# Split products in the first part's layer two, and a gather of the second part's rows in one stretch

## The chip, the core and the metric

The kernel runs on one core of a Trainium2 chip. The time is device microseconds of one execution, from launch to end; the figure for a kernel is the median of its runs. A separate execution was recorded by the hardware profiler, and all views of the trace come from that one.

## What is computed

The reference is one transformer block on x of shape (8, 1024, 512), float32: an attention whose queries, keys and values are sines and cosines of angles, and then a mixture of experts on the normalised result. Only the second half matters here:

```python
probs = softmax(x @ Wr + br)                 # E = 8 experts
topk_p, topk_e = top_k(probs, 2)
cap = 160                                    # places for each expert and batch entry
buf = scatter rows of x to (expert, batch, place)          # (8, 1280, 512)
h = relu(einsum('enc,ech->enh', buf, W1) + b1)             # 512 -> 2048
y = einsum('enh,ehc->enc', h, W2) + b2                     # 2048 -> 512
out = x + sum over a token's two places of gate * y
```

## The kernel before

**Parts.** Each expert has 1280 rows, taken as a part of 768 rows and a part of 512: sixteen parts, numbered from 0 (`chunks`). A part is cut in two halves of 384 or 256 rows, so `nh`, the number of row blocks of 128 in a half, is 3 or 2. For each part, layer one makes `hid` from the gathered rows (`xe` and its sums `xe_s`), then layer two makes the output rows `y` from `hid` and `w2`, and these are scaled by their gates and added to the output in memory by indirect DMA. All matrix products are float32, and a matmul instruction of the program shows as two records in the profile.

**Products.** Both layers multiply 2 by 2 blocks with seven products in place of eight. The price is sums of blocks. For `w2` they are made by `mix_w2` (VectorE, L1070, 32 instructions for an expert); for layer one's weights by `mix_w1` (L1233); for the rows by the last lines of `gather` (L1200 to L1203).

**Layer two** has three forms. `layer2` (L1372) takes one row block and runs the seven products plainly, each as eight matmuls of 256 columns. `layer2_quad` serves the 512-row parts. `layer2_six` serves 768-row parts from the third part on: product one of blocks 0 and 1 runs plainly (`pair_product`, L1540), the other six are split once more by the class `Second` into seven chains of four matmuls of 128 columns (L1491), and block 2 runs by `layer2`, a step at a time, between them (`some(1, extra)`). Each split product needs eight more sums of 128x512 on VectorE, four of weights (L1460) and four of rows (L1471), written by `both()` two products ahead. `run` then issues the chains, with copies out of PSUM on ScalarE (L1500 to L1515) and additions on VectorE (L1507 to L1513). The six run in the order 5, 6, 2, 3, 7, 4. Their sums alternate between two sets of room: the tiles `xe` and `xe_s`, and three `t1` tiles with `xg`.

The first part (i = 0) does not use it. Its three blocks run one after the other by `layer2`.

**Order.** The order of instructions on TensorE, VectorE, ScalarE and SP is the order in which the program writes them. Work of the next part is woven in by generators: `gather(i + 1, room)` is the generator `aside`, of which `some(n, aside)` or `next(aside)` writes n steps. POOL issues the indirect DMAs: the slot scatters (L773), the row gathers in `fetch` (L1097), and the sends of output rows (L1336).

**Rows.** `fetch` gathers 128 rows to SBUF, `put_row` (SP, L1108) writes them back to memory as `rows_d`, and `quarters` (SP, L1117) reads them again in four loads in a layout that VectorE turns with a 32 by 32 transpose (L1187). For the second part `find_rows(1)` (L1085) computes the row numbers from the slots, four blocks are fetched into the room of `xe_s`, put, and read back into two `z` tiles, two blocks early and two when a `z` comes free. In the first part `find_rows(1)` is written at the ninth step of the layer's 21. For later 512-row parts, `gather` gets `room`, two pieces of `hid` that are no longer read; blocks two and three are read into these.

**Pools** that matter: `ps_p`, six PSUM banks; `gp`, two `z` tiles and one `xg`; `yp`, five `y` tiles of 128x512, each for an output block's rows of one half, free when its send has landed.

Of the kernel before, what the change touches and what calls it, by code (L numbers as in the profile page):

```python
# [22 lines left out]
P = 128  # L23
# [51 lines left out]
def preln_attn_moe_kernel(  # L75
# [110 lines left out]
    room = [t[:, i, :].rearrange("p (i s) -> p i s", i=2) for i in range(2)]  # L186
# [547 lines left out]
    def some(count, *gens):  # L734

        for gen in gens:
            while count and next(gen, 0) is None:
                count -= 1
# [342 lines left out]
    def find_rows(i):  # L1081

        js = slice(chunks[i][1], chunks[i][1] + 2 * chunks[i][2])
        lo, hi = REACH[i]
        nc.vector.tensor_scalar(  # L1085
            source[:, :, js], meta[:, :, js, 0], float(hi * S), float(lo * S),
            ALU.min, ALU.subtract,
        )
# [4 lines left out]
    early = {}  # L1093

    def fetch(i, j, xg):
        e, j0, _ = chunks[i]
        ins = nc.gpsimd.indirect_dma_start(  # L1097
            out=xg, out_offset=None, in_=xn2_d[i % 2],
            in_offset=bass.IndirectOffsetOnAxis(ap=source[:, e, j0 + j, None], axis=0),
        )  # L1100
        if i in (1, 2):
            tc.keep_in_program_order(ins)
        return xg

    def put_row(i, j, xg):
        if i not in rows_d:
            rows_d[i] = dram.tile([2 * chunks[i][2] * P, D], F32, name=f"rows_d{i}")
        nc.sync.dma_start(rows_d[i][j * P : (j + 1) * P, :], xg)  # L1108
# [4 lines left out]
    def quarters(i, j, z):  # L1113

        src = rows_d[i].rearrange("(t g r) (a f) -> t a r g f", r=QUAD, g=NG, a=NG)[j]
        for a in range(NG):
            nc.sync.dma_start(  # L1117
                by_groups(z)[a * QUAD : (a + 1) * QUAD], src[a]
            )
        return z  # L1120
# [4 lines left out]
    def new_z():  # L1125
        return pools["gp"].tile([P, D], F32, name="z")
# [10 lines left out]
    def gather(i, room=None):  # L1137

        e, j0, nh = chunks[i]
        if i == 0:  # L1140
            there = []

            t = row2.tile([P, NCH, 2 * P], F32, name="xT", bufs=1).rearrange("p c t -> p (c t)")
            places = [row2.tile([P, D], F32, name="xn2") for _ in range(2)]
            places += [t[:, :D], t[:, D:]]
            there = [fetch(0, j, xg) for j, xg in enumerate(places)]
            yield None
            there += [fetch(0, 4, new_xg()), fetch(0, 5, new_z())]
        if room:
            spots = room  # L1150
            there = early.pop(i) + [quarters(i, j, room[j - 2]) for j in range(2, 2 * nh)]
            yield None
        xe = pools["xep"].tile([P, NCH, 2, HALF], F32, name="xe")

        def sums():
            return pools["xep"].tile([P, 3, 2, HALF], F32, name="xe_s")

        if not room:
            s = sums()
            spots = s.rearrange("p k c n -> p (k c n)")  # L1160
            spots = [spots[:, k * D : (k + 1) * D] for k in range(4)]
        if i == 1:
            for j, xg in enumerate(spots):
                put_row(1, j, fetch(1, j, xg))
            early[1] = [quarters(1, j, new_z()) for j in range(2)]
            yield None
        if i and not room:
            there = early.pop(i)
            if i > 1:
                there += [quarters(i, j, spots[j - 2]) for j in range(2, 2 * nh)]  # L1170
            yield None
            yield None
        for j in range(2 * nh):
            if j:
                yield None
            xg = there[j]
            dst = xe[:, :, j // nh, j % nh * P : (j % nh + 1) * P]
            if i == 0:
                ps = two_banks()[:, :, : NCH * 64]
                for c in range(NCH):  # L1180
                    by_halves(ps[:, :, c * 64 : (c + 1) * 64], xg[:, c * P : (c + 1) * P])
                nc.vector.tensor_copy(
                    dst.rearrange("p c (a q) -> p c a q", a=2),
                    ps.rearrange("p a (c q) -> p c a q", q=64),
                )
            else:
                nc.vector.transpose(  # L1187
                    dst.rearrange("p k (g j) -> p k g j", j=QUAD),
                    by_groups(xg).rearrange("p g (r k) -> p k g r", k=NCH),
                )  # L1190
            if len(there) < 2 * nh:
                there.append(quarters(i, len(there), new_z()))
        if room:
            yield None
            s = sums()
        n = nh * P
        a11, a12 = xe[:, :2, 0, :n], xe[:, 2:, 0, :n]
        a21, a22 = xe[:, :2, 1, :n], xe[:, 2:, 1, :n]
        s2, s3, s4 = (s[:, k, :, :n] for k in range(3))
        TT(s3, a11, a21, ALU.subtract)  # L1200
        TT(a21, a21, a22, ALU.add)
        TT(s2, a21, a11, ALU.subtract)
        TT(s4, a12, s2, ALU.subtract)  # L1203
        yield a11, a12, s4, a22, a21, s2, s3

    def behind(count, gen):
        for _ in range(count):
            yield
        yield from gen

    def later_on(do, *args):
        do(*args)
        yield

    def start(gen, box):
        for box[0] in gen:
# [140 lines left out]
    def new_y():  # L1357
        y = pools["yp"].tile([P, D], F32, name="y")
        return y, y[:, :DC], y[:, DC:]
# [164 lines left out]
    two = range(2)  # L1524
# [20 lines left out]
    def layer2_six(i, hid, aside, mix_next):  # L1545
# [28 lines left out]
        some(1, extra)  # L1574
        add_to(y11, second[2].run(c))
        second[7].both()
        three = second[3].run(c)
        for b in two:
            TT(as_pair(y12[b]), five[b], three[b], ALU.add)
# [9 lines left out]
        for b in two:  # L1589
            TT(as_pair(y22[b]), five[b], seven[b], ALU.add)  # L1590
        TT(c6, c6, c, ALU.add)
        some(1, aside)
        four = second[4].run(c5, lambda: some(2, aside), lambda: some(1, aside))
        for b in two:
            TT(as_pair(y21[b]), six[b], four[b], ALU.add)
# [106 lines left out]
    def experts(ending):  # L1702
# [5 lines left out]
        for i, (e, j0, nh) in enumerate(chunks):  # L1708
# [28 lines left out]
                    mixes = mix_w2(0)  # L1737
            rest(mixes)
            rest(ahead)
            room = [hid[:, 4 * h : 4 * h + 4, 0, :P] for h in range(2)] if i and nh > 2 else None  # L1740
            aside = start(gather(i + 1, room), box) if i + 1 < len(chunks) else iter(())
            if i == 0:

                aside = itertools.chain(behind(8, later_on(find_rows, 1)), aside)

            def mix_next():
                if i + 1 < len(chunks):
                    mix_w1(i + 1, 0)

            if i and nh > 2:  # L1750
                layer2_six(i, hid, aside, mix_next)
            elif i:
                layer2_quad(i, hid, second, aside, mix_next)
            else:
                for block in range(nh):
                    if block == nh - 1:
                        mix_next()
                    for _ in layer2(i, block, hid):
                        next(aside, None)
            rest(aside)  # L1760
            if i % 2 and e + 1 < E:
                load_b2(e + 1)
# [242 lines left out]
```

## Time and profile before

| | us |
|---|---|
| median of three runs | 3160.34 |
| lowest and highest | 3158.16, 3162.79 |
| profiled execution | 3160.96 |
| its span, first to last instruction | 3159.2 |
| TensorE busy in the span | 3085.4 |
| VectorE busy | 2393.9 |
| ScalarE busy | 1686.1 |
| first part's layer two, first matmul to the second part's first | 1333.95 to 1407.25 |
| third part's layer two, likewise | 1573.89 to 1642.61 |
| mean granted TensorE clock | 0.998 of full |

In the lines of the profile, PE is TensorE, PEld its weight loads, DVE VectorE, ACT ScalarE, POOL GpSimd, SP SyncE; a q behind the name is the engine's queue, which waits or issues. A line of the timeline gives the start, the time to the end of the last one, the engine, the line of the code, the operation, what is written and read, the shape, and how many there are in a row; in brackets the idle time before it and what ended it. A line of the windows gives for a stretch its length and for each engine the busy time and the number of instructions, then the granted TensorE clock, the mean share of the DMA engines and GB/s. Ends of matmuls are modelled, so lengths of TensorE's work are taken from start to start.

### The profile page before, as it was taken

What the parts mean: (1) busy time and instruction counts of PE and PEld (TensorE: products, weight loads), DVE (VectorE), ACT (ScalarE), POOL (GpSimd) and SP (SyncE); (2) the same over time, 40 slices, a digit from 0 to 9 for tenths busy, and PEclk for the clock granted to TensorE, in tenths of its full rate; (3) what the DMA queues carried; (4) which work ended last, traced back from release to release, by engine and by line L of the source; (5) the groups of instructions that cost most, each with busy time, mean ns of one, the idle gap of its engine ahead of it and who ended that gap; (6) DMA issues with size and microseconds to landing.
All of it is one profiled execution on the core that took longest, in us unless ns stands there. A gap on an engine that the chain in (4) does not pass through costs nothing.

```text
span 3159.2 us, 53457 instructions
## 1 busy us (share of the span) xinstructions
PE 3085.4 (98%) x20422; PEld 2149.6 (68%) x20422; DVE 2393.9 (76%) x4962; ACT 1686.1 (53%) x2672; POOL 421.3 (13%) x387
## 2 busy tenths in 40 slices
PE   5999999999999999999999999999999999999998
PEld 2454444544444544689699699699698698698697
DVE  8888888888888776738678678677777777777775
ACT  7888888888788885413423423423423423423423
POOL 3000202010101122320110110010110010110110
PEclk9999999999999999999999999999999999999999
DMA  5435454544545352433523523523523523423421
GB/s 168 148 101 167 110 165 133 156 135 147 155 140 161 81 168 63 142 84 96 156 52 92 156 50 99 155 50 99 150 54 102 142 57 105 135 57 108 133 46 22
DMA packets 288559, 358.86 MB, mean 114 GB/s; under 512 B 28376, under 2 KB 199088, under 8 KB 276272
## 3 DMA queue, kind: packets, MB, share of 16 engines
q1 hardware_dynamic: 264944, 312.20, 33.4%
q0 software_dynamic: 22912, 43.22, 7.5%
q8 instruction: 162, 2.65, 0.4%
q14 instruction: 93, 0.76, 0.1%
q10 hardware_dynamic: 448, 0.02, 0.0%
HBM read 207.02 MB, written 81.22 MB: 91 GB/s over the span
## 4 chain that ended last, share of the span: by engine, by line
PE 75%; ACT 12%; DVE 7%; DMA 3%; issue 2%; SPq 0%; POOLq 0%; POOL 0%; ACTq 0%; DVEq 0%
PE ps_p L1258 30%; PE ps_p L1491 13%; PE ps_s L688 8%; PE ps_p L1372 8%; PE ps_p L1540 7%; PE av L722 7%; ACT e L708 6%; ACT qk_c L598 1%; DMA xn_d<-xn 1%; ACT t_r L449 1%; PE ps_s L216 1%; ACT qk_r L449 1%; ACT L598 1%; DMA qk<-qk_r 1%; ACT L1908 1%
## 5 line engine op out<-in xcount | busy, mean ns | idle before, releaser
L688 PE MATMUL ps_s<-qk 64*128 64x512 f32 (+3 forms) x3072 | 584.6, 503 | 31.3 <-ACT e L708 13.7
L708 ACT ACTIVATE e<-ps_s 128x1024 f32<-128x1024 f32 (+1 forms) x640 | 554.4, 944 | 73.4 <-PE ps_s L702 45.3
L722 PE MATMUL av<-e,v 128*64 128x512 f32 (+3 forms) x3072 | 509.5, 488 | 0.0
L688 PEld LDWEIGHTS ps_s<-qk 64*128 64x128 f32 x3072 | 261.1, 188 | 219.1 <-ACT e L708 105.9
L722 PEld LDWEIGHTS av<-e,v 128*64 128x64 f32 x3072 | 206.0, 137 | 278.9 <-issue 258.5
L1258 PE MATMUL ps_p<-xe,w 128*128 128x256 f32 (+1 forms) x1024 | 317.6, 433 | 1.1 <-issue 1.1
L1258 PE MATMUL ps_p<-xe_s,t 128*128 128x256 f32 (+1 forms) x1024 | 317.7, 433 | 0.0
L1258 PE MATMUL ps_p<-xe,t 128*128 128x256 f32 (+1 forms) x1024 | 317.7, 433 | 0.0
L1336 POOL DMA_INDIRECT out_dram<-y,slots x80 | 127.6, 1595 | 1237.2 <-ACT y L1331 956.8
L773 POOL DMA_INDIRECT slot_d<-token,slot x128 | 153.6, 1200 | 1026.2 <-issue 627.2
L1258 PEld LDWEIGHTS ps_p<-xe_s,t 128*128 128x128 f32 x1024 | 194.4, 190 | 81.4 <-issue 0.8
L1258 PEld LDWEIGHTS ps_p<-xe,t 128*128 128x128 f32 x1024 | 194.2, 190 | 80.4 <-issue 0.4
L1258 PEld LDWEIGHTS ps_p<-xe,w 128*128 128x128 f32 x1024 | 193.7, 190 | 79.4 <-issue 1.2
L1301 DVE TENSOR_TENSOR hid<-hid 128x256 f32<-128x256 f32 (+1 forms) x128 | 63.5, 496 | 199.3 <-ACT hid L1299 199.1
L1258 PE MATMUL ps_p<-xe_s,w 128*128 128x256 f32 (+1 forms) x512 | 158.9, 433 | 0.6 <-ACT p L1274 0.6
L1372 PE MATMUL ps_p<-w,hid 128*128 128x256 f32 x640 | 142.9, 379 | 0.0
L1491 PE MATMUL ps_p<-w,hid 128*128 128x128 f32 x1104 | 141.8, 275 | 0.0
L702 PEld LDWEIGHTS <-keys_b 64*128 64x128 bf16 x1536 | 78.7, 95 | 91.1 <-issue 72.4
L730 DVE TENSOR_SCALAR av_sb<-av,inv_o 128x512 f32<-128x512 f32 x128 | 94.4, 746 | 57.7 <-PE av L722 57.6
L1491 PEld LDWEIGHTS ps_p<-w,hid 128*128 128x128 f32 x1104 | 135.3, 192 | 1.9
L1372 PEld LDWEIGHTS ps_p<-w,hid 128*128 128x128 f32 x640 | 121.1, 190 | 16.4
L1268 ACT COPY hid<-ps_p 128x256 f32<-128x256 f32 (+1 forms) x128 | 53.9, 421 | 139.4 <-PE ps_p L1258 127.4
(314 smaller groups left out, 5502.3 us busy)
## 6 DMA issues: line engine op xcount, KB each, us to landing
w<-in_L_ffn_W_dram SPq DMA_DIRECT2D x256, 256.0 KB, 3.5
w<-in_L_ffn_W_dram SPq DMA_DIRECT2D x64, 512.0 KB, 6.6
qk<-qk_c SPq DMA_DIRECT2D x124, 256.0 KB, 4.6
qk<-qk_r SPq DMA_DIRECT2D x120, 256.0 KB, 5.2
qk_base<-base_d SPq DMA_DIRECT2D x28, 1024.0 KB, 6.5
xn_d<-xn SPq DMA_DIRECT2D x72, 256.0 KB, 2.4
rows_d<-xg SPq DMA_DIRECT2D x70, 256.0 KB, 2.1
x_mid<-in_L_attn_x_dram SPq DMA_DIRECT2D x16, 1024.0 KB, 9.9
```

The lines of the kernel that those rows point to most:

```text
L688: nc.tensor.matmul(ps[:, a, at : at + w], lhsT=pair[r, 1, kb * P : (kb + 1) * P], rhs=pair[r, 0, q0 : q0 + w], start=at == 0, stop=not own ...
L702: nc.tensor.matmul(out_, lhsT=keys_b[r, part, :], rhs=late, start=False, stop=part == 1, skip_group_check=True,)
L708: nc.scalar.activation(e, ps[:, :, :n], AF.Exp, scale=UNIT * UNIT / math.sqrt(2 * DH))
L722: nc.tensor.matmul(av[a * 64 : (a + 1) * 64, q0 - 512 * h :], lhsT=vt[:, kb, 2 * pr + a, :], rhs=es[i][:, a, at : at + w], start=kb == 0, ...
L730: nc.vector.tensor_scalar(av_sb, av, inv_o[:, q : q + 1], None, ALU.mult)
L773: queued = nc.gpsimd.indirect_dma_start(out=slot_d[b], out_offset=bass.IndirectOffsetOnAxis(ap=idx, axis=0), in_=src, in_offset=None,)
L1258: nc.tensor.matmul(ps, lhsT=weights[:, k, :], rhs=rows[:, k, :], start=first and k == 0, stop=last and k == 1, skip_group_check=True,)
L1301: TT(g1, g3, h22, ALU.add)
L1336: ins = nc.gpsimd.indirect_dma_start(out=out, out_offset=bass.IndirectOffsetOnAxis(ap=meta[:, e, jj[r], 0:1], axis=0), in_=y, in_offset=No ...
L1372: nc.tensor.matmul(ps, lhsT=hid[:, k, part, cols], rhs=ws[weight][:, k, :], start=first and k == 0, stop=last and k == NHQ - 1, skip_group ...
L1491: nc.tensor.matmul(ps, lhsT=left[:, k, :], rhs=right[:, k, :], start=first and k == 0, stop=k == 3, skip_group_check=True,)
L1540: nc.tensor.matmul(of(ps, b), lhsT=hid[:, k, part, b * P : (b + 1) * P], rhs=ws[weight][:, k, :], start=first and k == 0, stop=last and k ...
```

## The change

The first part's layer two now goes through `layer2_six` as that of the other 768-row parts does. `gather` for the second part gets `room` as well: at its first step it computes the row numbers, fetches four blocks one after the other (two into `z` tiles, two into `y` tiles), puts them, reads blocks zero and one back into `z` and blocks two and three into the two pieces of `hid`. The step is written behind the sums of product seven. In `layer2_six` the first step of `aside` moves to that place for all parts, from behind product seven's additions; the other steps stay where they are.

```diff
         if room:
-            spots = room
+            if i == 1:
+                find_rows(1)
+                for j in range(2 * nh):
+                    put_row(1, j, fetch(1, j, new_z() if j < 2 else new_y()[0]))
+                early[1] = [quarters(1, j, new_z()) for j in range(2)]
             there = early.pop(i) + [quarters(i, j, room[j - 2]) for j in range(2, 2 * nh)]
             yield None
...
-        if i == 1:
-            for j, xg in enumerate(spots):
-                put_row(1, j, fetch(1, j, xg))
-            early[1] = [quarters(1, j, new_z()) for j in range(2)]
-            yield None
...
         second[7].both()
+        some(1, aside)
         three = second[3].run(c)
...
         TT(c6, c6, c, ALU.add)
-        some(1, aside)
         four = second[4].run(c5, lambda: some(2, aside), lambda: some(1, aside))
...
-            room = [hid[:, 4 * h : 4 * h + 4, 0, :P] for h in range(2)] if i and nh > 2 else None
+            room = [
+                hid[:, 4 * h : 4 * h + 4, 0, :P] for h in two
+            ] if nh > 2 else None
             aside = start(gather(i + 1, room), box) if i + 1 < len(chunks) else iter(())
-            if i == 0:
-
-                aside = itertools.chain(behind(8, later_on(find_rows, 1)), aside)
-
             def mix_next():
                 if i + 1 < len(chunks):
                     mix_w1(i + 1, 0)
 
-            if i and nh > 2:
+            if nh > 2:
                 layer2_six(i, hid, aside, mix_next)
-            elif i:
+            else:
                 layer2_quad(i, hid, second, aside, mix_next)
-            else:
-                for block in range(nh):
-                    if block == nh - 1:
-                        mix_next()
-                    for _ in layer2(i, block, hid):
-                        next(aside, None)
```

The helpers `behind` and `later_on`, which only the first part used, are removed.

## The prediction

> **What bounds the kernel now.** I read the page first (busy shares, slices, the chain that ended last), then the windows of two stretches, then the timelines of TensorE, VectorE, POOL and SP there.
>
> ```profile
> PE 3085.4 (98%) x20422; PEld 2149.6 (68%) x20422; DVE 2393.9 (76%) x4962; ACT 1686.1 (53%) x2672; POOL 421.3 (13%) x387
> ...
> PE 75%; ACT 12%; DVE 7%; DMA 3%; issue 2%; SPq 0%; POOLq 0%; POOL 0%; ACTq 0%; DVEq 0%
> ```
>
> TensorE is busy 98% and holds 75% of the chain. From the first expert on it has hardly a gap, so time saved or lost on it in the first part's layer two reaches the end one for one. That stretch is 1333.95 to 1407.25. The same step of the third part (second expert, 768 rows, already in six split products) is 1573.89 to 1642.61. The windows of both (PE, PEld, DVE, ACT, POOL busy, clock, DMA):
>
> ```profile
> 1333.95:1407.25 73.30, 72.78 (x337) 63.76 (x336) 25.88 (x54) 10.15 (x21) 22.68 (x21) 1.00 0.30 65
> 1573.89:1642.61 68.72, 68.72 (x481) 64.95 (x480) 54.72 (x104) 15.30 (x45) 7.34 (x5) 1.00 0.18 32
> ```
>
> The third part is the model of what the first becomes: 68.72 us on a TensorE without a gap, while VectorE does 54.72 us of work instead of 25.88.
>
> **TensorE's work.** For blocks 0 and 1 each of products two to seven loses 16 matmuls of 256 columns and gets seven chains of four matmuls of 128. Each matmul makes two records. The timeline of the third part:
>
> ```profile
> 1573.89 7.07 PE L1540 MATMUL ps_p<-w,hid 128*128 128x256 f32 x32
> 1580.79 1.05 PE L1491 MATMUL ps_p<-w,hid 128*128 128x128 f32 x8
> 1581.68 1.06 PE L1491 MATMUL ps_p<-xe,hid 128*128 128x128 f32 x8
> 1582.58 1.06 PE L1491 MATMUL ps_p<-xe 128*128 128x128 f32 x8
> ```
>
> Start to start, 16 wide matmuls take 6.90 us and a chain 0.893, so a split product takes 6.25. Six times 0.65 is 3.9 us less. Block 0's own small stall goes too (VectorE's sum L1415 holds TensorE, 0.7 us with the restart). Together that is the difference of the windows: 73.30 - 68.72 = **4.6 us gained**, if the sums keep up.
>
> **The sums of product five come late.** VectorE is strictly in order, and the sums (L1460, L1471) stand behind the mixture of the weights (L1070). In the first part the mixture runs on into layer two:
>
> ```profile
> 1343.67 0.43 DVE L1070 TENSOR_TENSOR w_t<-w,w_t 128x256 f32<-128x256 f32 x1
> 1344.02 0.41 DVE L1389 TENSOR_TENSOR y<-y,ps_p 128x256 f32<-128x256 f32 x1
> ```
>
> In the third part it is over before, and the sums start 3 us ahead of TensorE's first split chain (1577.91 against 1580.79):
>
> ```profile
> 1577.91 1.29 DVE L1460 TENSOR_TENSOR xe<-w 128x512 f32<-128x512 f32 x2
> 1579.11 0.69 DVE L1471 TENSOR_TENSOR xe<-hid 128x512 f32<-128x512 f32 x1
> 1579.84 0.69 DVE L1471 TENSOR_TENSOR hid<-hid 128x512 f32<-128x512 f32 x1
> ...
> 1587.19 0.68 DVE L1471 TENSOR_TENSOR xg<-hid,t 128x512 f32<-128x512 f32 x1
> 1587.80 0.28 DVE L1507 TENSOR_TENSOR xe_s<-xe_s,ps_p 128x128 f32<-128x128 f32 x1
> ```
>
> Today nothing splits here, so nobody waits for 1344.02. After the change: product one ends at 1333.95 + 6.90 = 1340.85, the first chain (no sums) at 1341.75. The second needs the fourth sum, done 2.62 us after the first starts (1580.53 - 1577.91): 1344.02 + 2.62 = 1346.64. TensorE stands **4.9 us**. Its third chain needs the sixth sum (3.82 after the start, 1347.84), 0.3 more. Sixteen sums (9.9 us) then stand before the first PSUM addition of product five. It runs at 1353.9; the next addition on VectorE frees ScalarE's last copy of product five, and behind that stand product six's copies. Product six's third chain can start at about 1354.95 instead of 1354.2, 0.75 more. Together **6.0 us lost**. Later sets have slack: product two starts near 1366.3 (1340.85 + 6.0 + two products at 6.25 + 6.90 of block 2) and its sums are done by 1360.
>
> **The fetch in one stretch.** `find_rows(1)` moves behind the sums of product seven. In the third part these end 12.0 us after product two starts (1612.36 - 1600.33), so here at 1378.3, against 1365.73 before. Behind it stand VectorE's additions of product three; the slots landed at 1365.5, so it waits for nothing. POOL's four gathers follow, now ahead of all six sends, which have nothing ready before them. Then SP's four puts and sixteen quarter loads, no longer waiting for z buffers. From the start of a `find_rows` to its first gather is 0.96 us (1165.48 to 1166.44 at the first part), and from there:
>
> ```profile
> 1371.84 1.01 POOL L1097 DMA_INDIRECT xe_s<-xn_d,source  x1 [0.30 <-issue]
> 1373.15 0.97 POOL L1097 DMA_INDIRECT xe_s<-xn_d,source  x1 [0.30 <-issue]
> 1374.43 0.94 POOL L1097 DMA_INDIRECT xe_s<-xn_d,source  x1 [0.30 <-issue]
> ```
>
> ```profile
> 1378.37 0.32 SPq L1108 DMA_DIRECT2D rows_d<-xe_s  x1
> ```
>
> The third put leaves 6.5 us after the first gather and lands 2.1 us later (the row rows_d<-xg of the DMA list): 1379.2 + 6.5 + 2.1 = 1387.8.
>
> That put matters because row blocks two and three now sit in y buffers. The pool has five; three are in use, these two fill it, and block 2's second y, next in order, inherits the first of them. In the built order of the changed kernel ScalarE's copy into it (L1395) waits for exactly that put. In the third part this copy runs at 1613.20, here it could at 1379.2, so ScalarE stands 8.6 us. Queued behind it: the copy L1397, two gates of block rows 0 and 1, and product seven's first copy, 0.27 + 0.27 + 0.62 + 0.62 + 0.27 = 2.05 us, done at 1389.8. TensorE's third chain of product seven waits for that copy and is due at 1366.3 + 21.2 = 1387.5. **2.3 us lost**. Bounds: the gather lands in 3.2 to 7.7 us and the put in 1.9 to 9.5, so 1 to 6; I take the pace of the same four rows, being nearest.
>
> The rows themselves are in time: first transpose 12.3 us after the first gather (1384.11 - 1371.84), at 1391.5, and it is wanted behind product seven's additions, after 1395. So I cost the sixteen quarter loads and SP's later w1 loads at nothing; the cover is some 4 us. In later parts only the moment of one step's writing moves; its loads keep their place in SP's queue and wait for TensorE's reading of `hid` (84.7 us over seven waits): 0.
>
> **The clock.** Windows around the two places where the granted clock fell:
>
> ```profile
> 58.00:61.40 3.40, 0.48 (x8) 0.20 (x4) 3.40 (x3) 3.37 (x4) 0.00 (x0) 1.00 0.56 231
> 61.40:64.80 3.40, 2.62 (x6) 1.39 (x8) 3.37 (x3) 2.57 (x4) 0.00 (x0) 0.50 0.98 231
> 64.80:68.20 3.40, 3.40 (x10) 1.62 (x8) 2.71 (x4) 2.04 (x3) 0.00 (x0) 0.50 1.04 268
> ...
> 832.80:836.20 3.40, 1.49 (x14) 0.89 (x16) 3.10 (x5) 0.00 (x0) 0.00 (x0) 1.00 0.95 363
> 836.30:839.60 3.30, 3.30 (x30) 0.98 (x30) 0.38 (x3) 2.05 (x2) 0.00 (x0) 0.50 0.05 20
> ```
>
> After 3.4 us with 0.48 us of TensorE work the clock was 0.50 for 6.8 us, after 3.4 with 1.49 for 3.4. Half clock costs half of that time, 1.7 to 3.4 us. The 4.9 us stall leaves some such stretch idle for over 2.4 us wherever its edges fall, so I count a drop; its 1.7 to 3.4 covers the 0.3 and 0.75 above, leaving about 1.3. The Trainium skill (TensorE: Matmul & The Clock Gate, "Why this matters for your kernels") says to leave no gap over about 3 us, since one idle window brings half clock. By that rule the 2.3 us stall costs nothing more and the sum is 5.0. By the row 832.80, under half busy was enough, and a 2.3 us stall lies in one stretch that far in about 6 cases of 10: 0.6 x 1.7 = 1.0. I take the row.
>
> A second rule speaks against the change: SBUF — State Buffer, "Who interferes with whom", has a VectorE instruction with two SBUF inputs contend with GpSimd's reads. The new sums run beside POOL's slot scatters. In the trace these step by 2.4 to 3.0 us beside VectorE's mixture (1336.73 to 1344.62) and 2.37 beside an idle VectorE. Eight at 0.6 more land the slots at 1370.5, still before 1378.3: 0.
>
> **Sum.** -4.6 + 6.0 + 2.3 + 1.3 + 1.0 = +6.0 us. The profiled execution took 3160.96 (span 3159.2 and 1.8 around it), 0.6 over the median of three, 3160.34. On the median: **3166.3**.
>
> **Rivals.**
> - The gain stands: -4.6, 3155.7. One place decides: if VectorE is through the mixture by 1339.1 instead of 1344.0, the fourth sum is there at 1341.75 and the stalls at five and six go, and with an earlier fetch the put hides. Against it: the mixture's rows follow each other without a gap from 1339.3 on, and nothing ahead of them is changed. 0.05.
> - Only the sums stall, and a quick put or an intact clock hides the rest: +1.4 to +3, about 3162.5. For it: the gather's shortest landing. 0.13.
> - The rows come too late: the gather runs 7 us later, and if loads and sends collide by over 4 us, transposes, the four sums and the first product of the second part slip behind TensorE's arrival: +9 to +14, about 3172. For it: landings up to 9.5 us. Against: no weights load in that stretch. 0.20.
> - The change does less than it says: excluded, the built order has 168 more narrow and 96 fewer wide matmuls.
>
> **Numbers.** The forecast has 0.62, its own range 3163.5 to 3169. Range for 8 in 10: 3161 to 3172. 0.2%, 6.3 us, is about what a measurement of this kernel can tell from no change; my value lies at that edge, so the forecast splits nearly evenly. Slower: half of 0.62 less a little plus 0.20, 0.49. Same: the rest of it, 0.13 and most of the first rival, 0.49. Faster: 0.02.
>
> **What would show it.** TensorE idle about 4.9 us before the second chain of product five, released by VectorE L1471; 0.50 clock behind it; ScalarE idle some 8 us at L1395, released by a put; product seven's third chain late by about 2 us. I am wrong if the stretch from product one to the second part's first matmul is under 73.3 us, or if a wait for rows or z at the second part's start appears.

## The result, and the profile after

| | before | after |
|---|---|---|
| median of 12 runs each, us | 3161.13 | 3168.18 |
| lowest and highest | 3158.16, 3164.06 | 3163.99, 3171.86 |
| profiled execution, its span | 3160.96, 3159.2 | 3171.37, 3169.6 |
| first part's layer two (start to start on TensorE) | 73.30 | 81.33 |
| second part's layer one, likewise | 48.35 | 50.48 |

The ratio of the times is 1.0024, with an interval of 1.0015 to 1.0033: the changed kernel is slower by 5 to 10 us. A second set of runs, told of below, gave 1.0033 (1.0021 to 1.0046). The profiled execution of after is 3.2 us above its own median, so the traces differ by more (10.4 us of span) than the medians do (7.1).

On the page of after, TensorE is as busy as before (3085.9 against 3085.4 us), though the change takes work from it. At half clock the same work takes longer (a chain of product five 2.08 us instead of 1.05, below), and the record counts that as busy:

```profile
PE 3085.9 (97%) x20566; PEld 2155.2 (68%) x20566; DVE 2429.0 (77%) x5032; ACT 1690.9 (53%) x2696; POOL 422.4 (13%) x387
...
PE 75%; ACT 12%; DVE 7%; issue 3%; DMA 3%; SPq 0%; POOL 0%; POOLq 0%; ACTq 0%; DVEq 0%
```

The windows of the two stretches that differ (length, then PE, PEld, DVE, ACT, POOL busy, clock, DMA share, GB/s). What comes ahead of them, and every later layer, has its length of before within 0.4 us:

```profile
1333.57:1414.90 81.33, 73.67 (x482) 69.59 (x481) 62.31 (x124) 15.42 (x45) 23.22 (x20) 0.94 0.25 57
...
1414.90:1465.38 50.48, 49.12 (x226) 42.35 (x225) 34.73 (x87) 23.51 (x62) 9.54 (x8) 1.00 0.53 142
```

In the first, TensorE has 482 records, against 481 in the third part, which has no gap, but it lies idle 7.66 us of 81.33 and its mean clock is 0.94. Of the lines quoted here, those with numbers under 1150 are as in before, L1186 is its L1187, and the later ones are ten lower: L1481 is before's L1491, L1461 its L1471, L1385 its L1395.

**The stall of the sums.** The timeline of VectorE and of TensorE at product five of the changed kernel:

```profile
1343.29 0.42 DVE L1070 TENSOR_TENSOR w_t<-w,w_t 128x256 f32<-128x256 f32 x1
1343.63 1.28 DVE L1450 TENSOR_TENSOR xe<-w 128x512 f32<-128x512 f32 x2
1344.83 0.69 DVE L1461 TENSOR_TENSOR xe<-hid 128x512 f32<-128x512 f32 x1
1345.56 0.69 DVE L1461 TENSOR_TENSOR hid<-hid 128x512 f32<-128x512 f32 x1
```

```profile
1340.47 1.05 PE L1481 MATMUL ps_p<-w,hid 128*128 128x128 f32 x8
1346.30 2.08 PE L1481 MATMUL ps_p<-xe,hid 128*128 128x128 f32 x8 [4.78 <-DVE hid L1461]
```

The sums begin when the last instruction of the weight mixture is done, and TensorE starts its second chain at the end of the fourth sum. The 2.08 us of that chain, twice the 1.05 of the one before it, is the half clock. Windows cut at the records of the clock:

```profile
1342.20:1345.61 3.41, 0.00 (x0) 0.00 (x0) 3.27 (x8) 0.00 (x0) 2.00 (x2) 1.00 0.01 0
1345.61:1349.02 3.41, 2.72 (x12) 2.72 (x13) 3.41 (x6) 0.27 (x1) 1.27 (x2) 0.50 0.01 1
1349.02:1352.44 3.42, 3.42 (x18) 3.42 (x17) 3.39 (x7) 0.27 (x1) 1.35 (x2) 0.50 0.01 0
```

From the end of the gap at 1346.30 to 1352.44 TensorE works at half speed: 6.14 us, half of it lost, 3.07.

**The stall at the put.** ScalarE and TensorE at product seven:

```profile
1390.00 0.37 ACT L1385 COPY y<-ps_p 128x256 f32<-128x256 f32 x1 [9.19 <-DMA rows_d<-y]
1390.27 0.38 ACT L1387 COPY y<-ps_p 128x256 f32<-128x256 f32 x1
1390.54 1.34 ACT L1321 ACTIVATE y<-y,slots 128x512 f32<-128x512 f32 x2
1391.77 0.26 ACT L1490 COPY xe_s<-ps_p 128x128 f32<-128x128 f32 x1
```

```profile
1388.14 1.06 PE L1481 MATMUL ps_p<-xe,hid 128*128 128x128 f32 x8
1392.09 1.16 PE L1481 MATMUL ps_p<-xe 128*128 128x128 f32 x8 [2.89 <-ACT xe_s L1490]
```

ScalarE stands 9.19 us for the third put, then works off what was queued behind it, and TensorE's third chain waits for the last of that. Another half clock follows (1393.40 to 1396.81), 1.7 us lost.

The account of layer two closes: 73.30 - 4.5 (the work saved) + 4.78 + 3.07 + 2.89 + 1.70 = 81.24, against 81.33.

**A third loss, in the second part's layer one.** TensorE, VectorE and POOL there, one fence for each:

```profile
1460.09 1.13 PE L1248 MATMUL ps_p<-xe_s,t 128*128 128x256 f32 x4 [1.19 <-ACT hid L1258]
```

```profile
1455.62 0.43 DVE L1223 TENSOR_TENSOR t<-w 128x256 f32<-128x256 f32 x1 [1.29 <-DMA w<-in_L_ffn_W_dram]
```

```profile
1412.00 1.55 POOL L1326 DMA_INDIRECT out_dram<-y,slots  x1 [3.91 <-issue]
1418.54 1.55 POOL L1326 DMA_INDIRECT out_dram<-y,slots  x1 [4.99 <-ACT hid L1268]
1424.60 1.55 POOL L1326 DMA_INDIRECT out_dram<-y,slots  x1 [4.51 <-ACT hid L1288]
1426.45 1.22 POOL L1097 DMA_INDIRECT xg<-xn_d,source  x1 [0.30 <-PE ps_p L1248]
```

Read from the end backwards: VectorE's mixture of layer one's weights (L1223) waits for a w1 load. On SP that load stands behind a put of the third part's rows (L1108). The put waits for a gather on POOL (L1097), and the gather stands behind the sends of output rows, which come one at a time, some 6 us apart. The last send is 9.7 us into the second part (1424.60 - 1414.90) and the gather 11.6; before the change, where the part begins at 1407.25, they were 4.8 and 6.6 us in:

```profile
1412.02 1.55 POOL L1336 DMA_INDIRECT out_dram<-y,slots  x1 [4.08 <-DMA out_dram<-y,slots]
1413.87 1.01 POOL L1097 DMA_INDIRECT xg<-xn_d,source  x1 [0.30 <-issue]
```

SP shows the result, first after, then before:

```profile
1397.11 23.51 SPq L1047 DMA_DIRECT2D w<-in_L_ffn_W_dram  x4
1430.71 0.34 SPq L1108 DMA_DIRECT2D rows_d<-xg  x1
1431.17 1.24 SPq L1047 DMA_DIRECT2D w<-in_L_ffn_W_dram  x2
```

```profile
1418.71 0.34 SPq L1108 DMA_DIRECT2D rows_d<-xg  x1
1419.16 1.24 SPq L1047 DMA_DIRECT2D w<-in_L_ffn_W_dram  x2
```

The w1 pair behind the first put goes out at 1431.17, 16.3 us into the part; before it went out at 1419.16, 11.9 us in. Each later pair stands behind the next put in the same way.

### The profile page after: what moved, and what is told of

It is laid out like the page before. It is cut to its first block, busy times and chain, and to the rows that moved or that the text cites. A ratio compares the mean times of both kernels' runs of the same rounds, so it can differ in the third digit from the quotient of the medians.

```text
span 3169.6 us, 53852 instructions
## 1 busy us (share of the span) xinstructions
PE 3085.9 (97%) x20566; PEld 2155.2 (68%) x20566; DVE 2429.0 (77%) x5032; ACT 1690.9 (53%) x2696; POOL 422.4 (13%) x387
## 4 chain that ended last, share of the span: by engine, by line
PE 75%; ACT 12%; DVE 7%; issue 3%; DMA 3%; SPq 0%; POOL 0%; POOLq 0%; ACTq 0%; DVEq 0%
PE ps_p L1248 30%; PE ps_p L1481 14%; PE ps_s L688 8%; PE av L722 7%; PE ps_p L1530 7%; ACT e L708 6%; PE ps_p L1362 6%; DMA xn_d<-xn 1%; PE ps_s L216 1%; ACT qk_c L598 1%; ACT t_r L449 1%; ACT qk_r L449 1%; DMA qk<-qk_r 1%; ACT L598 1%; ACT L1890 1%
## 5 line engine op out<-in xcount | busy, mean ns | idle before, releaser
L1481 PE MATMUL ps_p<-w,hid 128*128 128x128 f32 x1152 | 149.1, 276 | 0.0
L1481 PEld LDWEIGHTS ps_p<-w,hid 128*128 128x128 f32 x1152 | 142.1, 193 | 2.0
L446 ACT ACTIVATE qk_f<-qk_f,split_c 128x1024 f32<-128x1024 uint16 (+1 forms) x66 | 70.5, 1115 | 105.7 <-DVE qk_r L442 105.7
L1248 PEld LDWEIGHTS ps_p<-xe_s,w 128*128 128x128 f32 x512 | 97.2, 190 | 41.5 <-ACT p L1264 1.2
```

The costliest lines, as they stand in the source:

```text
L446: nc.scalar.activation(p.bitcast(F32), f, AF.Square, bias=split_c, scale=1.0 / FINE)
L1248: nc.tensor.matmul(ps, lhsT=weights[:, k, :], rhs=rows[:, k, :], start=first and k == 0, stop=last and k == 1, skip_group_check=True,)
L1481: nc.tensor.matmul(ps, lhsT=left[:, k, :], rhs=right[:, k, :], start=first and k == 0, stop=k == 3, skip_group_check=True,)
```

## The experiments

All are edits of the changed kernel (after), run in groups, each group beside runs of the kernel before. "Layer two" is the first part's and "layer one" the second part's, both in the experiment's own profile.

| kernel | ratio to before (interval) | layer two | layer one |
|---|---|---|---|
| after, again | 1.0033 (1.0021 to 1.0046) | 81.21 | 50.62 |
| own y | 1.0033 (1.0021 to 1.0045) | 79.51 | 52.58 |
| fetch early | 1.0012 (1.0003 to 1.0020) | 74.98 | 51.39 |
| block 2 first | 1.0012 (1.0004 to 1.0020) | 74.30 | 52.55 |
| rows later | 1.0023 (1.0014 to 1.0032) | 80.02 | 48.35 |
| filled gaps | 1.0025 (1.0016 to 1.0035) | 77.70 | 51.89 |
| one product first | 1.0010 (1.0004 to 1.0017) | 74.54 | 50.43 |
| block 2 first, fetch early | 0.9995 (0.9987 to 1.0003) | 68.80 | 50.63 |
| the same and rows later | 0.9988 (0.9981 to 0.9994) | 68.80 | 48.35 |
| fetch alone | 1.0030 (1.0018 to 1.0042) | 81.42 | 48.35 |
| fetch alone, spaced | 1.0008 (0.9999 to 1.0016) | 73.30 | 49.06 |

A difference of some 1.5 us in the column of layer two can be the clock's alone. "Rows later" leaves layer two as in after, with gaps of 4.77 and 2.96 us, and took 80.02 against 81.33: the half clock behind product five lasted 3.4 us there and 6.8 in after.

**Is it VectorE's lateness? Block 2's products first.**

```diff
             nc.scalar.copy(y11[b], of(top, b))
+        if i == 0:
+            some(1, extra)
+            some(1, extra)
         second[6].both()
...
-        some(1, extra)
+        if i:
+            some(1, extra)
         second[3].both()
-        some(1, extra)
+        if i:
+            some(1, extra)
```

> For the first part, the first two plain products of block 2 (6.9 us on TensorE, with no sums of VectorE behind them) are written right behind product one instead of around the sums of product three; all work is the same. Theory 1 (the gap of 4.78 us before product five's second chain is VectorE being late with sums that stand behind the mixture of w2, and the half clock behind it comes from that gap): the gap goes, the clock stays at 1.00 there, the start of product two falls from 34.3 to between 26.4 and 27.5 us after the first matmul, apart from the 6.9 us of block 2 that moves ahead of it in both; in all 7 to 8 us less in the stretch. The later gap at product seven stays, 2 to 4 us, since the fetch then comes at about the same distance from the sums. Rival A (VectorE is short of time throughout, since the split doubles its work): the gap moves to product six or two, and the gain is under 3 us. Rival B (the gap is for PSUM or for ScalarE's copies): it stays, and the gain is nil.

Measured: layer two 74.30, 7.0 less than after. TensorE's timeline shows block 2's product in the place of the gap, and the next two chains at their pace of 0.89 us with the clock at 1.00:

```profile
1338.22 7.07 PE L1362 MATMUL ps_p<-w,hid 128*128 128x256 f32 x32
1345.13 1.05 PE L1481 MATMUL ps_p<-w,hid 128*128 128x128 f32 x8
1346.02 1.06 PE L1481 MATMUL ps_p<-xe,hid 128*128 128x128 f32 x8
```

The gap at product seven stayed (3.69 us, with its half clock). The same work in another order costs nothing at product five or later, so VectorE is not short of time over the whole; it is late at one place. Rivals A and B fall. The account closes here too: 81.33 - 4.78 - 3.07 + 0.80 (the later gap is that much longer) = 74.28.

**How much late? One product first.** Only one of the two `some(1, extra)` is moved.

> As the experiment that moves two plain products of block 2 right behind product one, but only the first of them (3.45 us of TensorE) is moved; the other stays behind the sums of product three. Theory 1 (TensorE waits for sums that are late by a fixed time, and every us of other work put ahead takes one off): the gap before product five's second chain is 4.78 - 3.45 = 1.3 us, and no half clock follows[...]; the stretch of layer two is then 81.3 less 3.45 and less 1.7 to 3.1 of half clock, some 75 to 76.5, and the gap at product seven stays at 2.9 to 3.7. Rival (the gap comes from an order of waits, not from time: a semaphore or a bank set free by a certain instruction): it keeps its 4.8 us or goes altogether.

Measured: the gap is 1.34 us, as 4.78 - 3.45 says, and layer two took 74.54, with the clock at 1.00 throughout, 0.2 us above what moving both gave (which had a half clock at product seven).

```profile
1345.57 1.16 PE L1481 MATMUL ps_p<-xe,hid 128*128 128x128 f32 x8 [1.34 <-DVE hid L1461]
```

So each us of other work put ahead takes one us off the gap. I expected 75 to 76.5: I had left the half clock behind the second gap in that number, and here that gap, 2.94 us long, brought none. The windows, cut at whole steps of 3.413 us from this run's clock records, show what differed: its idle time was shared between two of them.

```profile
1381.60:1385.01 3.41, 1.63 (x15) 1.44 (x13) 0.59 (x2) 0.92 (x3) 0.00 (x0) 1.00 0.62 231
1385.01:1388.43 3.42, 2.25 (x20) 2.26 (x21) 0.10 (x1) 1.54 (x5) 1.64 (x1) 1.00 0.71 137
```

In after, TensorE was busy 1.31 of 3.4 us in the window before the second drop:

```profile
1390.00:1393.40 3.40, 1.31 (x11) 1.32 (x12) 0.00 (x0) 2.32 (x7) 1.65 (x1) 1.00 0.58 175
```

**Does the half clock cost anything? Filled gaps.**

```diff
             chain(u, a11, b11, True)
             nc.scalar.copy(c11, u)
+            filler(fill[0])
             between()
             chain(v, a21, t1, True)
             nc.scalar.copy(c21, v)
+            filler(fill[1])
...
-        five = second[5].run(c5)
+        five = second[5].run(c5, fill=(0 if i else 10, 0))
...
-        seven = second[7].run(c)
+        seven = second[7].run(c, fill=(0, 0 if i else 6))
```

> In the first part, ten extra matmuls of 256 columns are issued after the first chain of product five and six after the second chain of product seven; their results are not used. They keep TensorE busy where it stands idle in the changed kernel (4.78 and 2.89 us), at about 0.43 us each, and wait for nothing. Theory 1 (each stall costs its length and besides a half clock of 3.4 to 6.8 us behind it): the granted clock stays at 1.00 through the stretch, which falls from 81.33 (80.02 in the last experiment's profile) by the 2 to 4.8 us lost to the half clock, less about 1 us of the sums' lateness that comes to the fore at product six: 77 to 78.5. The runs also lie closer together. Rival (the half clock is hidden: TensorE would wait for late sums at product six anyway, or the clock falls for another reason): clock 0.50 still seen, or the stretch stays at 80 to 81.

Measured: no 0.50 in the stretch, which took 77.70. The fillers (L1491 in this kernel's lines, two records each) left 0.46 us of the gap at product five, and the sums' lateness came up at product six, as expected:

```profile
1335.57:1413.27 77.70, 76.55 (x514) 70.95 (x512) 61.90 (x124) 15.20 (x45) 22.42 (x20) 1.00 0.25 59
```

```profile
1343.37 4.48 PE L1491 MATMUL ps_t<-w,hid 128*128 128x256 f32 x20
1348.31 1.16 PE L1481 MATMUL ps_p<-xe,hid 128*128 128x128 f32 x8 [0.46 <-DVE hid L1461]
...
1356.59 1.16 PE L1481 MATMUL ps_p<-t,t 128*128 128x128 f32 x8 [0.49 <-ACT xe_s L1500]
```

TensorE does 32 records more and is 3.6 us sooner through the stretch than in after. So the half clock is a cost of its own, on top of the gaps: 3.07 and 1.70 us in after, less about 1.1 us of the sums' lateness that it had covered (0.4 at product five's third chain, 0.7 at product six's). Two things did not come as expected. The runs do not lie closer together (3163.96 to 3172.79), so these two drops are not what spreads them. And the whole kernel is not measurably faster than after: layer one was 1.4 us longer, and the rest is within the interval.

**Is it the wait for the put? Own y.** Block 2's second y is taken before the gather takes its two.

```diff
-        yield
+        if i:
+            yield
         y2, y21, y22 = new_y()
         nc.scalar.copy(y22, mid)
+        if i == 0:
+            yield
```

> For the first part, block 2's second y buffer is taken, and the copy into it written, before the gather takes its two y buffers, so ScalarE's copy inherits no buffer that a put still reads. The new wait of ScalarE at L1385 (for the third put) goes. Theory 1 (that wait holds ScalarE, and through it product seven's first copy and TensorE): the gap of 2.89 us before product seven's third chain goes, and with it the half clock behind it (3.41 us at 0.50, 1.7 us of loss): the stretch from product one to the second part's first matmul is 81.3 - 4.6 = 76.7 us. The sends keep their pace, one behind the other's landing, so the second part's layer one may wait up to 4.6 us longer for its w1 loads: the whole is 1 to 4 us below the changed kernel. Rival (ScalarE is only a bystander, the gap is late sums of product seven or a clock matter): the gap stays within 0.5 us of 2.89 and the stretch at 81.

Measured: layer two 79.51, where I expected 76.7. ScalarE no longer waits for a put and the gap at product seven's third chain is gone (1388.19, in step with its neighbours). But the pool has five y whoever takes which. Now product seven's outputs inherit them: VectorE (L1584) waits for a send and then for a put, and TensorE follows, some 4 us later in the stretch than in after. (The edit moves these lines down by three.)

```profile
1396.16 0.42 DVE L1584 TENSOR_TENSOR y<-xe_s 128x256 f32<-128x256 f32 x1 [3.90 <-DMA out_dram<-y,slots]
1396.84 0.48 DVE L1584 TENSOR_TENSOR y<-xe_s 128x256 f32<-128x256 f32 x1 [0.25 <-DMA rows_d<-y]
```

```profile
1396.99 1.23 PE L1484 MATMUL ps_p<-t,t 128*128 128x128 f32 x8 [2.38 <-ACT xe_s L1493]
```

This gap of 2.38 us has a half clock of 3.4 us behind it, as the old one had. So of the 1.8 us that layer two gained, only 0.5 is the gap; the other 1.4 is the half clock at product five, which lasted 3.4 us in this run and 6.8 in after. Layer one took 2.1 us more than in after, and the whole is no faster. That the wait for the put holds TensorE stands, the remedy doesn't: what is short is the time between the fetch and the next use of its buffers.

**The time of the fetch. Fetch early.**

```diff
         second[3].both()
+        if i == 0:
+            some(1, aside)
         some(1, extra)
...
         second[7].both()
-        some(1, aside)
+        if i:
+            some(1, aside)
```

> For the first part, the gather step (row numbers, four fetches, four puts, loads) is written behind the sums of product three instead of those of product seven, some 10 us earlier on VectorE. Theory 1 (the time of the fetch sets the wait for the put, and its place ahead of the sends sets when the last sends, the third part's gather and puts, and SP's later w1 loads come): the put lands near 1378, before ScalarE needs the buffer; the gap of 2.89 us and the half clock behind it go (-4.6); the sends begin some 5 us earlier (about 1386) and the waits in the second part's layer one shrink by 1 to 2 us. Together 5 to 6.5 us below the changed kernel. Rival A (the fetch and its quarter loads cost by their own traffic, wherever they stand): nothing changes by more than 1 us. Rival B (the slots are not yet there, or the fetch collides with the slot scatters): VectorE or POOL waits at the new place and the stretch grows.

Measured: layer two 74.98. The put is no longer in ScalarE's way; the copy into block 2's second y runs without a wait:

```profile
1373.82 0.38 ACT L1385 COPY y<-ps_p 128x256 f32<-128x256 f32 x1
```

The gap at product five is unchanged (4.78), so the two stalls are independent; its half clock was 1.4 us here. Rivals A and B fall. But layer one did not improve: 51.39. My expectation that an earlier fetch lets the sends begin earlier was wrong. They begin when their rows are done: the first send waits 12.33 us for the gate of its rows (L1321).

**The third loss. Rows later.** The fetch and the puts of the third part's rows, one step later in SP's order.

```diff
-                next(ahead, None)
+                if i != 1 or q:
+                    next(ahead, None)
```

> In the second part's layer one, the fetch and the puts of the third part's rows are written one step later, behind more of SP's w1 loads. Nothing is changed in the first part. Theory 1 (the 2.1 us lost in the second part's layer one are SP's w1 loads standing behind puts that wait for POOL's fetches, which stand behind six sends, each of them waiting for the landing of the one before): the gaps at 1452.6 and 1460.1 go, layer one of the second part takes 48.4 instead of 50.5 us, the rest is unchanged, and the whole is about 2 us below the changed kernel, unless the later rows hold up the third part. Rival (layer one is slower because of the traffic of the sixteen late quarter loads or of the late sends themselves): it stays at 50.5 us.

Measured: layer one 48.35, as before the change, without a gap, while the last send came at the same place (9.3 us into the part). SP now has six loads ahead of the first put:

```profile
1395.89 29.20 SPq L1047 DMA_DIRECT2D w<-in_L_ffn_W_dram  x6
1430.26 0.34 SPq L1108 DMA_DIRECT2D rows_d<-xg  x1
```

Traffic as the cause falls. The whole cannot show 2 us against after: the intervals overlap. In the other kernels with the sends of the six products and the puts in their old place, layer one follows the moment of the first gather: 11.4 to 11.8 us into the part gives 50.4 to 50.6, 11.9 gives 51.39, 13.2 gives 51.89, 13.6 and 13.8 give 52.55 and 52.58.

**Two, then all three mended.** Block 2 first and fetch early together:

> The two moves of earlier experiments together: two plain products of block 2 right behind product one, and the gather step behind the sums of product three. Theory 1 (the two stalls are independent, each with its own cause): layer two of the first part loses both gaps and takes 68.7 to 69.7 us, as the third part does, with the clock at 1.00. But the sends keep their pitch of landing after landing, so the shorter stretch is partly given back in the second part's layer one, which takes 53 to 55 us instead of 51.4 and 52.6 in the two alone; the whole is 0 to 2 us above the kernel before at most, or up to 1 below. Rival (layer one's wait depends on the moment of the fetch, not on the sends): layer one takes at most 51.4 us, and the whole is 2 us or more below the kernel before.

Measured: layer two 68.80, clock 1.00. The wait for the put is hidden and not gone: ScalarE still stands 4.06 us for it, since block 2's products, moved ahead, bring its copy closer to the fetch, but it is through with what is queued before product seven's first chain has ended.

```profile
1379.65 0.37 ACT L1385 COPY y<-ps_p 128x256 f32<-128x256 f32 x1 [4.06 <-DMA rows_d<-y]
```

Layer one 50.63, not 53 to 55: the loss there belongs to the order of sends and not to the length of layer two, so what is saved in layer two isn't given back. That part of my theory was wrong, and the length of layer one is on the rival's side. But the rival's reason isn't it either: with the same early fetch alone it was 51.39, and in both kernels the last send came late into the part (9.5 and 10.1 us), as in after (9.7). Then with the third part's rows later:

> As the one before, and besides in the second part's layer one the fetch and puts of the third part's rows are written one step later. Theory 1 (the three losses of the change are the stall of the sums, the stall at the put with the half clocks of both, and SP's w1 loads behind puts): all are gone, the split's own 4.6 us of TensorE's work are left as a gain: layer two of the first part 68.7 to 69.7, layer one of the second 48.4, the whole 3.5 to 4.6 us below the kernel before. Rival (the loss comes back a step further on, with the third part's rows or weights later by one step): a new gap in the second part's later products or at the third part's start, and the whole no better than the kernel before.

Measured: 3156.5 us, median of 21 runs, against 3160.62 before (39 runs). This version beats both kernels, that of before by 4 us of 3160, with an interval of 2 to 6. The two stretches have no idle time on TensorE at all:

```profile
1333.32:1402.12 68.80, 68.80 (x482) 64.95 (x480) 61.66 (x124) 15.65 (x45) 23.53 (x20) 1.00 0.29 66
1402.12:1450.47 48.35, 48.35 (x226) 42.56 (x225) 34.41 (x87) 24.62 (x62) 9.50 (x8) 1.00 0.55 148
```

The gain is the split's own: 73.30 - 68.80 = 4.5 us. No later layer is longer than before by more than 0.1 us, so the loss doesn't come back further on. The cover at the put is thin: ScalarE stands 4.59 us for it in this run, and is ready 0.47 us before product seven's first chain gives it the next copy.

**The changed kernel once more.**

> The changed kernel itself again, on the same chip as the three others, for a comparison in the same rounds and a second profile. Theory 1: both gaps (4.8 and about 2.9 us) and the waits in the second part's layer one at the same places; the half clocks behind the gaps last 3.4 or 6.8 us, by where the gap falls, so the stretch varies between 79 and 82 us; the whole 7 to 8 us above the kernel before.

Measured: gaps of 4.78 and 3.01 us, half clock for 6.8 and 3.4 us behind them, 81.21 and 50.62. The ratio was 1.0033.

**The other half alone. Fetch alone.** The first part by plain products again, the fetch in one stretch at the ninth step.

```diff
-            if nh > 2:
+            if i and nh > 2:
                 layer2_six(i, hid, aside, mix_next)
-            else:
+            elif i:
                 layer2_quad(i, hid, second, aside, mix_next)
+            else:
+                aside = itertools.chain(iter([None] * 8), aside)
+                for block in range(nh):
+                    if block == nh - 1:
+                        mix_next()
+                    for _ in layer2(i, block, hid):
+                        next(aside, None)
```

> Half of the change alone: the first part's layer two by plain products, three blocks one after the other, as in the kernel before; but the second part's rows are fetched in one stretch with two z and two y buffers, at the ninth step, where the row numbers were computed before. Theory 1 (the fetch in one stretch costs nothing by its own traffic; in the changed kernel it costs because it comes late, behind the sums): TensorE has no new gap in layer two, which takes 73.3 us with 0.3 either way; block 2's second y waits for a put that has long landed; layer one of the second part takes 48.4 to 49.5; the whole within 1.5 us of the kernel before. Rival (sixteen quarter loads and four puts at once hold up sends, weights or rows): layer two or the second part's layer one is longer by 2 us or more, with gaps behind DMA.

Measured: layer two 81.42, a miss, and neither theory had it. VectorE's order put the first transpose right behind the fetch:

```profile
1364.55 0.18 DVE L1085 TENSOR_SCALAR source<-slots 128x32 int32<-128x32 int32 x1 [3.69 <-DMA slots<-slot_d]
1383.13 1.08 DVE L1186 STREAM_TRANSPOSE xe<-z 128x512 f32<-128x512 f32 x1 [18.40 <-DMA z<-rows_d]
```

```profile
1386.57 1.65 PE L1362 MATMUL ps_p<-w_t,hid 128*128 128x256 f32 x3 [5.45 <-DVE y L1395]
```

From row numbers to rows on the chip the fetch takes 18.6 us. The first 5.8 of them the gathers stand behind two sends on POOL (the first runs at 1370.33); four gathers, four puts and the loads take the other 12.8. VectorE waits for it in order, and TensorE behind VectorE. So this run isn't a measure of the fetch. With six empty steps before the transposes:

```diff
-                aside = itertools.chain(iter([None] * 8), aside)
+                six = iter([None] * 6)
+                aside = itertools.chain(
+                    iter([None] * 8), itertools.islice(aside, 1), six, aside
+                )
```

> As the experiment with the fetch in one stretch and plain products, with six empty steps put between the step that fetches and the first 32 by 32 transpose, so that VectorE comes to the transposes some 20 us later. In the run without them VectorE stood 18.4 us at the first transpose, for rows that landed 18.6 us after the row numbers. Theory 1 (the fetch in one stretch costs nothing in itself; what costs is an instruction in VectorE's order that comes before the rows have landed): the 5.45 us gap and the half clock go, layer two takes 73.3 to 73.8 us, the second part's layer one 48.4, and the whole is within 1.5 us of the kernel before. Rival (the traffic of the fetch costs, or its four z and y buffers do): layer two stays 2 us or more above 73.3, with another wait.

Measured: layer two 73.30, to the hundredth that of before, and the transposes start without a wait:

```profile
1383.16 2.08 DVE L1186 STREAM_TRANSPOSE xe<-z 128x512 f32<-128x512 f32 x2
```

The fetch in one stretch is free in layer two when nothing in order stands in front of its landing. Layer one was 0.7 us longer, a gap of 0.44 near its start among it. The empty steps also moved the sums of the rows (L1199 to L1202): the last ends at 1406.08, 0.7 us after the part begins, where in before it ended 8.2 us ahead, and the part's first weight sums (L1223) stand behind it. That this is the whole of the 0.7 is not shown. The interval of the time, 0.9999 to 1.0016, shows no difference from the kernel before.

## Why the prediction was right, point by point

- **TensorE's work, -4.6.** Right: 4.5 with all stalls taken away.
- **The sums of product five, 6.0.** The 4.9 us measured 4.78, at the instruction named. The 0.3 and 0.75 behind it did not appear beside the half clock. With the clock kept up, in the filled gaps and with one product first, they did: the third chain came 1.30 us after the second instead of 0.89, and product six's third chain 0.66 late, with TensorE idle for 0.49 of it. Start to start, product two began 34.27 us after product one, against 26.44 in the third part: 7.83 for sums and clock, where the sum had 6.0 + 1.3 = 7.3. The clock drop was 3.07 us in this run and 1.4 in another, by where the gap fell.
- **The put, 2.3.** Measured 2.89. The chain ScalarE, put, buffer was as described. The put landed just before 1390.0 instead of at 1387.8, while TensorE's third chain was due at 1389.03, 1.5 us later than reckoned too, which took most of it back. That the size came out so near is in part luck.
- **The second clock drop, 0.6 x 1.7 = 1.0.** It came in both profiles of after (1.7 each), and not in the run with one product first, after a gap as long. Weighing it by a chance was right in kind. The gaps in after, 2.89 and 3.01, are too near 3 us to decide between the row and the rule of about 3 us; the run with its own y speaks for the row, with half clock behind a gap of 2.38 us.
- **Slots beside the new sums, 0.** Right: `find_rows` had no wait in front of it.
- **"So I cost the sixteen quarter loads and SP's later w1 loads at nothing."** The first half was right. The second is the term that was mis-sized: 2.1 us. I had asked whether the quarters come in time for the transposes, and not what later sends on POOL do to the next gathers, the puts behind them on SP, and the loads behind the puts. (Four of the six sends were out by 1388.69 before; in after the first goes at 1391.55, when its rows are done.) The cover of 4 us that I named was for other work. The rows-later run shows it: one step moved, and the 2.1 us are gone.
- **Sum.** Terms -4.6, 7.3, 2.3 and 1.0 against -4.5, 7.85 (4.78 and 3.07), 2.89 and 1.7 measured, and 0 against 2.1: +6.0 was forecast, +10 is in the profile, +7 between the medians. 3168.18 lies in the forecast's own range of 3163.5 to 3169, nearer its upper end. That is in part luck: both profiles of after have +10 in these two stretches, and the second set of runs, 1.0033, is +10 too, which on 3160.34 lies above that range and inside the wider one of 3161 to 3172.
- **The rivals.** That the gain stands needed the mixture done at 1339.1; it was done at 1343.7. That only the sums stall did not happen either, with two gaps and two drops of the clock. That rows come too late did not happen: VectorE reached the first transpose at 1399.72 and did not wait.

## What to carry to other kernels

A change that saves work on the bounding engine is worth its saving only if the other engines' orders have room where it is put: here the same split brought +7 us where the weight mixture was still running and a fetch had its buffers in the way, and -4 us once 6.9 us of unrelated products stood in front of it, the fetch came earlier and the next rows' puts later. Work added to an in-order queue is to be followed until the next reader of everything behind it, also across the part's end: the last 2 us were lost three queues further on, in loads of the next part. And where a step fetches in the background, count from its first gather to its landing (12.8 us here, and 5.8 more behind two sends) and to the next use of every buffer that it takes.

## What the runs showed of the hardware that I had not expected

The clock is cut into stretches of 3.413 us: in the profile of after all changes of the clock are whole multiples of that apart. I took TensorE's busy time (its ends are modelled) in each stretch of all thirteen profiles. Coming back to full clock asks for more than I thought. In after the first half-clock stretch had 2.72 us of TensorE work, and the next was at half clock again; in the fetch-early run it had 2.85, and the next was whole:

```profile
1340.42:1343.83 3.41, 2.85 (x13) 2.85 (x14) 3.41 (x6) 0.27 (x1) 1.78 (x2) 0.50 0.01 0
1343.83:1347.25 3.42, 3.42 (x33) 3.42 (x32) 3.39 (x7) 0.53 (x2) 1.40 (x2) 1.00 0.01 0
```

The other profiles have no exception: half clock went on behind every such stretch with 2.72 us or less, and ended behind every one with 2.85 or more.

The fall has no such edge. Behind every full-clock stretch with 1.43 us of work or less came half clock (0, 0.92 and 1.31 in the two profiles of after), and behind none with more than 2.04. Between the two both were seen: with block 2 first and fetch early, 1.82 us of work at 1248.6 was followed by half clock; with the rows later besides, 1.82 at 1248.3 was not. So busy time in this form doesn't settle when the clock falls, and what else counts stays open.

The Trainium skill (TensorE: Matmul & The Clock Gate, Part 1: The HAM clock gate) has half clock after an idle window and full clock after a busy one, with free-running windows of this length. The runs agree on the length and on the windows running free. They add that a window need not be idle for the drop (1.31 us of work in after) nor busy throughout for the return (2.85). So the same 4.8 us gap cost 1.4 us of half clock or 3.1, by where it fell.
